# An attention and expert kernel: written order for its transfers, another opening, and another engine for the last sums

## The chip, the cores and the metric

The kernel runs on one core of a Trainium2 chip. The metric is the device time of one execution in microseconds (us). Three runs of the kernel before took 4551.12 to 4552.34 us, with a median of 4551.49 us.

A core has five engines, each with an instruction queue of its own: TensorE (PE in the profile, its weight loads PEld), VectorE (DVE), ScalarE (ACT), GpSimd (POOL) and SyncE (SP), which here only issues transfers. ScalarE and GpSimd issue transfers too.

## The reference, cut to what matters

```python
xn = layernorm(x)                          # x: (4, 2048, 512) float32
q, k, v = split(xn @ w_qkv, 3)             # 16 heads of 32
q, k = (irfft(rfft(t) * sigmoid(mask_logits)) for t in (q, k))
attn = softmax(einsum('bhqd,bhkd->bhqk', q, k) / sqrt(32))
attention = einsum('bhqk,bhkd->bhqd', attn, v).reshape(B, S, 512) @ w_out + b_out
best = argmax(softmax(xn @ w_gate))        # 8 experts, 100 tokens each
expert = gate * (xn @ w_expert + b_expert) # for the tokens that find a place
return x + attention + expert
```

The filter of q and k is linear, so the kernel multiplies the q and k weights by a filter matrix once, at the start.

## The kernel before, in words

**Units of work.** A stage k (0 to 15) is one batch and one group of four heads: b = k // 4, group c = k % 4. A stage has four blocks of 512 queries (n), a block has eight windows (w), and a window takes two tiles of 128 keys, an even and an odd one. So there are 512 windows of four passes (two tiles, two pairs of heads u). In each pass of the main loop (L844 to L892) TensorE does `shift` (L593: adds minus the row maxima, `negm`, into a PSUM bank by a bf16 matmul), the matmuls of one item of the maxima of a later block (`max_matmuls`, L446), and `scores` (L582). ScalarE takes the exponential into the tile `even` or `odd`, and VectorE reduces the maxima (`max_reduce`, L458, into `part`). `products` (L609) of the tile before multiplies by the values, and VectorE adds them into `num`.

**Maxima.** They run 40 items ahead (MAX_AHEAD), that is ten windows; a block has 32 items. The first 40 are worked off in a prelude before window 0 (L728 to L744). The last item of block B (numbered through, 0 to 63) falls in window 8B-3. `max_negate` (L470) then makes `neg` on VectorE, and in window 8B-2 `max_close` (L475) transposes it on TensorE, copies it to `rest` on ScalarE, splits it on GpSimd into three bf16 rows (`row`; a cast, then twice a subtraction and a cast) and has SP write these into `negm` by three DMAs. Block B begins in window 8B and can't before that. After window 501 there are no maxima left.

**Row sums.** For the denominators, the odd tile of a window is added onto the even one by an accumulating DMA from GpSimd's queue at the start of the next window (`pair`, L833), and the even tile of the window before onto that by GpSimd in the window after (`add_to`, L836, two instructions). After a block, `close_steps` (L628) makes the row sums on TensorE (`fold`), sends them through memory so that 128 partitions share the reciprocal (`sums`, `few`, `inverse`, `factor`: SP's DMAs, with the reciprocal of `few` on VectorE), multiplies on GpSimd (`ot`), projects, copies to `y` on ScalarE and adds `y` to the output by an accumulating DMA from GpSimd's queue (`add`, ten windows after the block). The very last block is closed by `close_last` (L673).

**Order.** Steps other than the passes stand in an agenda, a list for each window (`plan`, L782); half of them run after the even tile, half after the odd one. From L724 on, TensorE, VectorE, ScalarE and GpSimd are wrapped in `InOrder` (L71), which keeps their instructions in the written order. SP is not, nor is anything in the opening: there the framework's scheduler chooses the order of the queue. A DMA that waits in a queue holds up those behind it.

**Hand-over.** The tokens of the next batch are read twice, in chunks of 1 MB. In stage c = 2 they are loaded, measured, given the bias `b_out` and stored to the output as its first sum. From the end of that stage on they are loaded again, normalized and turned into `xnT`, in stage c = 3. Both passes use the two `xs` buffers of the pool `chunks`. The weights of a stage (`wg`, one buffer) are loaded from `wd` at the end of the stage two before it.

**Opening.** ScalarE's queue issues the constants, the raw weights and the V part of `wd` (L128 to L181), then comes the sigmoid (L182). SP loads x, and the filtering of group 0 (`filter_weights`, L192), which goes through `wd` in memory and back, stands behind the first chunk (L690 to L702). The other three groups are filtered in the prelude.

Of the kernel before, what the change touches and what calls it, by code (L numbers as in the profile page):

```python
# [25 lines left out]
P = 128  # L26
# [75 lines left out]
def attention_and_top1_experts(ctx: ExitStack, tc: tile.TileContext, a: dict, out: bass.AP):  # L102
# [24 lines left out]

    freq = const.tile([2 * NF, 2, P], F32, name="freq")  # L128
# [4 lines left out]
    falling = const.tile([P, E], F32, name="falling")  # L133
    nc.scalar.dma_start(out=falling, in_=a["c_falling"])
    token = const.tile([P, NT], F32, name="token")
    nc.scalar.dma_start(out=token, in_=a["c_token"])
    mask = const.tile([2 * NF, 1], F32, name="mask")
    logit_col = a["L0_attn_mask_logits"].rearrange("(f o) -> f o", o=1)
    nc.scalar.dma_start(out=mask[0:NF], in_=logit_col)
    nc.scalar.dma_start(out=mask[NF : 2 * NF], in_=logit_col)  # L140
# [30 lines left out]
    wd = [dram1.tile([P, NR, 3, P], F32, name=f"wd{c}") for c in range(NG)]  # L171
    raw = {}
    for s in range(2):
        for g in range(NR // 2):
            if g == 0:
                both = probs(s == 1)
            raw[s, g] = both[:, g]
            nc.scalar.dma_start(out=raw[s, g], in_=w_qkv[:, 2 * g : 2 * g + 2, s * DM : (s + 1) * DM])
    for c in range(NG):
        cols = slice(2 * DM + c * P, 2 * DM + (c + 1) * P)  # L180
        nc.scalar.dma_start(out=wd[c][:, :, 2, :], in_=w_qkv[:, :, cols])  # L181
# [9 lines left out]
    on = SimpleNamespace(tensor=nc.tensor, vector=nc.vector, scalar=nc.scalar, gpsimd=nc.gpsimd)  # L191
    def filter_weights(c):  # L192
        for s in range(2):
            pt, pw = bank(), bank()
            for r in range(NR):
                on.tensor.transpose(
                    pt[:, r * P : (r + 1) * P], raw[s, r // 2][:, r % 2, c * P : (c + 1) * P], ident
                )
            if s == 0:
                both = probs(c == 1)  # L200
            wt = both[:, s]
            on.scalar.copy(wt[:, 0, :], pt)
            for r in range(NR):
                at = slice(r * P, (r + 1) * P)
                on.tensor.matmul(pw[:, at], lhsT=wt[:, 0, at], rhs=filt, start=True, stop=True)
            on.scalar.copy(wt[:, 1, :], pw)
            nc.sync.dma_start(out=wd[c][:, :, s, :], in_=wt[:, 1, :].rearrange("p (r n) -> p r n", r=NR))
# [4 lines left out]
    def token_stage(b):  # L212
# [6 lines left out]
        def load(n, name="xs"):  # L219
            held[n] = chunk(name)  # L220
            nc.sync.dma_start(out=held[n], in_=x[b, n])
# [9 lines left out]
        def first_sums(n):  # L231

            nc.sync.dma_start(out=o[b, n], in_=held[n])

        def scale(first=0, last=NT):
            at = slice(first, last)
            on.scalar.activation(rstd[:, at], mv[:, at, 1], AF.Sqrt, bias=eps[:, 0:1])
            on.vector.reciprocal(rstd[:, at], rstd[:, at])
            on.gpsimd.tensor_tensor(shift[:, at], mv[:, at, 0], rstd[:, at], ALU.mult)
            on.gpsimd.tensor_scalar(shift[:, at], shift[:, at], -1.0, None, ALU.mult)  # L240
# [138 lines left out]
    wg, wo = {}, {}  # L379

    def load_qkv_weights(k):
        wg[k] = weights.tile([P, NR, 3, P], F32, name="wg", bufs=1)
        nc.sync.dma_start(out=wg[k], in_=wd[k % NG])

    def load_out_weights(k):
        c = k % NG
        wo[k] = weights.tile([P, DM], F32, name="wo")
        nc.sync.dma_start(out=wo[k], in_=a["L0_attn_w_out"][c * P : (c + 1) * P, :])
# [86 lines left out]
    def max_close(k, n):  # L475

        pn = bank()[0 : HG * TQ, 0:P]
        on.tensor.matmul(pn, lhsT=negs.pop((k, n)), rhs=ident, start=True, stop=True)
        rest = small.tile([HG * TQ, P], F32, name="rest")
        row = small.tile([HG * TQ, 3, P], BF16, name="row", bufs=2)  # L480
        on.scalar.copy(rest, pn)
        on.gpsimd.tensor_copy(row[:, 0, :], rest)
        for i in (1, 2):
            on.gpsimd.tensor_tensor(rest, rest, row[:, i - 1, :], ALU.subtract)
            on.gpsimd.tensor_copy(row[:, i, :], rest)
        negms[k, n] = qkv.tile([P, QB], BF16, tag="negm", name="negm", bufs=3)
        for i in range(3):
            nc.sync.dma_start(out=negms[k, n][i::DH, :], in_=row[:, i, :])
# [4 lines left out]
    def expert_steps():  # L493


        def begin():
            w_exp = chunk("w_exp")
            nc.sync.dma_start(out=w_exp, in_=a["L0_ffn_w_expert"].rearrange("(r p) n -> p r n", p=P))
            b_exp = work.tile([P, DM], F32, tag="b_exp", name="b_exp", bufs=1)
            nc.sync.dma_start(out=b_exp, in_=a["L0_ffn_b_expert"].partition_broadcast(P))  # L500
            entries = small.tile([P, NTAB, ST, 2], F32, name="entries")
            for i, table in enumerate(tables):
                nc.sync.dma_start(out=entries[:, i], in_=table.rearrange("(t p) c -> p t c", p=P))
# [124 lines left out]
    def close_steps(k, n, num, acc):  # L628
# [4 lines left out]
        def fold():  # L633
            den = work.tile([P, QB], F32, tag="den", name="den", bufs=1)
            on.scalar.copy(den, row_sums([acc]))
            held["sums"] = scratch.tile([HG, QB], F32, name="sums")
            nc.sync.dma_start(out=held["sums"], in_=den[0::DH, :])


        def fetch():  # L640
            held["few"] = small.tile([P, HG * QB // P], F32, name="few", bufs=2)
            nc.sync.dma_start(out=held["few"], in_=held["sums"].rearrange("h (c e) -> (h c) e", e=HG * QB // P))

        def invert():
            on.vector.reciprocal(held["few"], held["few"])
            held["inverse"] = scratch.tile([HG, QB], F32, name="inverse")
            nc.sync.dma_start(
# [3 lines left out]
        def spread():  # L651
            held["factor"] = work.tile([P, QB], F32, tag="factor", name="factor", bufs=1)
            for h in range(HG):
                nc.sync.dma_start(
                    out=held["factor"][DH * h : DH * (h + 1)], in_=held["inverse"][h].partition_broadcast(DH)
                )
# [12 lines left out]

        steps = [(2, fold), (3, fetch), (4, invert), (5, spread), (7, divide)]  # L670
        return steps + [(8, result, 0), (8, result, 1), (9, result, 2), (9, result, 3), (10, add)]

    def close_last(k, n, num, tiles, y):  # L673
# [9 lines left out]
        for t in range(TQ):  # L683
            on.vector.tensor_tensor(y[:, t, :], y[:, t, :], project(k, ot, t), ALU.add)
            if t % 2 == 1:
                nc.sync.dma_start(out=o[b, n, :, t - 1 : t + 1, :], in_=y[:, t - 1 : t + 1, :])
# [3 lines left out]
    for n in range(NQ):  # L690
        tiles = range(n * TQ, (n + 1) * TQ)
        load(n, "y" if n == 2 else "xs")
        for i in tiles:
            measure(i)
        scale(tiles[0], tiles[-1] + 1)
        for i in tiles:
            normalize(i)
            if i % 2 == 1:
                turn(i - 1)
        if n == 0:  # L700
            filter_weights(0)
            load_qkv_weights(0)  # L702
# [17 lines left out]
    first_projections = projections(0)  # L720
    for step in first_projections[:2]:
        step()
    ahead, first_projections = first_projections[2:7], first_projections[7:]
    on.tensor, on.vector, on.scalar, on.gpsimd = (  # L724
        InOrder(tc, engine) for engine in (nc.tensor, nc.vector, nc.scalar, nc.gpsimd)
    )
    closing = {}
    for i, item in enumerate(stream[:MAX_AHEAD]):  # L728
        if i % 4 == 0 and ahead:
            ahead.pop(0)()  # L730
        if i % 10 == 9 and i < 30:
            filter_weights(i // 10 + 1)
# [6 lines left out]
        max_reduce(item, half)  # L739
        while full_blocks:  # L740
            closing[i + 2] = full_blocks.pop(0)
            max_negate(*closing[i + 2])
        if i in closing:
            max_close(*closing[i])  # L744

# [36 lines left out]
    def plan(k):  # L782
# [18 lines left out]
        if k + 2 < B * NG:  # L801
            at(start + GW - 1, load_qkv_weights, k + 2)
# [3 lines left out]
        if c == NG - 2 and b + 1 < B:  # L806

            at(start + 10, begin_stage, b + 1)
            for n in range(NQ):
                at(start + 11 + 4 * n, in_stage, 0, n)  # L810
                at(start + 18 + 4 * n, in_stage, 7, n)
            for i in range(NT):
                at(start + 13 + i, in_stage, 1, i)
                at(start + 14 + i, in_stage, 6, i)
            at(start + GW - 2, in_stage, 2)
            at(start + GW - 2, in_stage, 0, 0)
            at(start + GW - 1, in_stage, 0, 1)
# [18 lines left out]
    def add_to(tile, sum_before):  # L836
        for u in range(2):
            on.gpsimd.tensor_tensor(tile[:, u], tile[:, u], sum_before[:, u], ALU.add)

    pairs, adds = {}, {}  # L840
# [3 lines left out]
    for k in range(B * NG):  # L844
        plan(k)
        for n in range(NQ):
            num = work.tile([P, QB], F32, tag="num", name="num")
            tiles = {}
            for w in range(NW):
                even, odd = w * WIN, w * WIN + 1  # L850
                if window in pairs:
                    pair(*pairs.pop(window))
                if window in adds:
# [3 lines left out]
                for j in (even, odd):  # L857
# [14 lines left out]
                    while full_blocks:  # L872
                        block = full_blocks.pop(0)
                        max_negate(*block)
                        at(window + 1, max_close, *block)
                    if left:
                        products(*left)
                    left = k, n, j, tiles[j], num
                    for step in here[:cut] if j == even else here[cut:]:
                        step()  # L880
                last = (k, n) == (B * NG - 1, NQ - 1)
                if not last or w < NW - 1:
                    pairs[window + 1] = tiles[even], tiles[odd]
                    if 0 < w and not (last and w == NW - 2):
                        adds[window + 2] = tiles[even], tiles[even - WIN]
                if last and w == NW - 2:
                    y = chunk("xs")
                    nc.sync.dma_start(out=y, in_=o[B - 1, n])
# [4 lines left out]
    products(*left)  # L893
    for step in agenda[window]:
        step()
    close_last(k, n, num, [tiles[j] for j in (NT - 6, NT - 4, NT - 2, NT - 1)], y)
# [36 lines left out]
```

## Time and profile before

| what | value |
|---|---|
| median of three runs | 4551.49 us |
| the profiled execution's own time | 4547.31 us |
| its span, first to last instruction | 4545.5 us |
| mean granted TensorE clock | 0.984 |
| DMA moved | 708.87 MB, mean 156 GB/s |
| first maxima matmul | 63.52 us |
| first matmul of window 0 | 123.84 us |
| last `products` matmul ends | 4512.2 us |
| `few` reciprocal, 128x16, VectorE | 247 ns |
| `row` cast, 16x128, GpSimd | 284 ns |
| `rest` subtraction, 16x128, GpSimd | 418 ns |
| `even` addition, 128x1024, GpSimd | 2549 ns |
| max reduction, 128x1024, VectorE | 1220 ns |

In the lines of the profile, a time line has start, duration, engine, source line, operation, out<-in, the shape and the count of merged instructions; in brackets stands the idle time before it and what ended it. L82 is the line of the `InOrder` helper and stands for every pinned instruction, so one goes by tile names there. SPq, ACTq and so on are the queues as they issue transfers. PEclk is the clock that TensorE was granted, as a share of full speed.

### The profile page before, as it was taken

To read this page: it belongs to the slowest core of one execution; us is meant where nothing else is said; L and a number is where in the kernel's file an instruction comes from. 1 tells how busy PE (TensorE), PEld (TensorE's weight loads), DVE (VectorE), ACT (ScalarE), POOL (GpSimd) and SP (SyncE) were. 2 spreads that over 40 slices of the span, in tenths; PEclk is the share of its full clock that TensorE was granted. 3 is DMA by queue.
4 is the path that set the end of the run, shared out by engine and by line. 5 is a ranking of instruction groups with operands and counts; after the bars stand their busy time and mean duration, and the time that the engine had idled before them with its cause. 6 is when DMAs were issued, how large, how long until landed. Compare 5 with 4: busy or idle time off the path is not lost.

```text
span 4545.5 us, 106083 instructions
## 1 busy us (share of the span) xinstructions
PE 4381.8 (96%) x44390; PEld 1877.2 (41%) x44390; DVE 3099.6 (68%) x3609; ACT 2590.4 (57%) x4933; POOL 3002.4 (66%) x2082
## 2 busy tenths in 40 slices
PE   6999999989999999998999999998999999999997
PEld 3444443434434344443444434343343444434332
DVE  4666777765767777775667767776667766777772
ACT  3455565565555655556555555555655565555654
POOL 0477676755766766775577666776567665777666
PEclk9999999999999999999999999999999999999998
DMA  5587787877777878797677777788768776788787
GB/s 119 132 176 154 148 161 151 193 174 145 151 149 144 163 154 160 154 211 171 125 150 149 160 152 146 163 175 181 162 127 159 155 148 128 152 171 163 153 166 146
DMA packets 193231, 708.87 MB, mean 156 GB/s; under 512 B 47778, under 2 KB 54084, under 8 KB 127344
## 3 DMA queue, kind: packets, MB, share of 16 engines
q0 software_dynamic: 110576, 606.88, 68.4%
q1 hardware_dynamic: 77800, 91.56, 6.6%
q8 instruction: 347, 5.69, 0.5%
q10 hardware_dynamic: 4376, 3.67, 0.4%
q14 instruction: 132, 1.08, 0.1%
HBM read 77.09 MB, written 89.99 MB: 37 GB/s over the span
## 4 chain that ended last, share of the span: by engine, by line
PE 85%; DMA 7%; POOL 3%; issue 2%; ACT 2%; DVE 1%; ACTq 0%; POOLq 0%; SPq 0%; DVEq 0%
PE array L82 85%; DMA even<-odd 3%; POOL even L82 2%; DMA few<-sums 1%; DMA negm<-row 1%; ACT odd L82 1%; DMA sums<-den 1%; DVE part L82 1%; DMA wg<-wd 0%; POOL ot L82 0%; DMA wd<-in_L_attn_w_qkv_dram 0%; ACT even L82 0%; PE array L394 0%; POOL table L82 0%; ACT xs L82 0%
## 5 line engine op out<-in xcount | busy, mean ns | idle before, releaser
L82 DVE TENSOR_REDUCE part<-array 128x2 f32<-128x1024 f32 (+1 forms) x2308 | 2432.7, 1099 | 1222.0 <-PE array L82 1210.0
L82 POOL TENSOR_TENSOR even<-even 128x1024 f32<-128x1024 f32 x892 | 2171.4, 2549 | 236.0 <-DMA even<-odd 234.1
L82 PE MATMUL array<-k,q 32*128 32x512 f32 x8192 | 2228.0, 623 | 1.9 <-DVE part L82 1.9
L82 PE MATMUL array<-q,k 32*128 32x512 f32 x8192 | 2057.8, 596 | 0.0
L82 ACT ACTIVATE even<-array 128x512 f32<-128x512 f32 x2048 | 1065.5, 601 | 501.6 <-PE array L82 484.5
L82 ACT ACTIVATE odd<-array 128x512 f32<-128x512 f32 x2048 | 1060.3, 601 | 442.1 <-issue 236.6
L82 POOL DMA_DIRECT2D even<-odd x511 | 464.0, 908 | 1059.9 <-ACT odd L82 865.4
L82 PEld LDWEIGHTS array<-k,q 32*128 32x128 f32 x8192 | 811.1, 184 | 175.1 <-DVE num L82 74.1
L82 PE MATMUL array<-negm,ones_b 3*128 3x512 bf16 x4096 | 799.4, 383 | 53.0 <-DMA negm<-row 35.5
L82 PEld LDWEIGHTS array<-q,k 32*128 32x128 f32 x8192 | 751.2, 186 | 11.4 <-issue 2.5
L82 DVE TENSOR_TENSOR num<-num,array 128x512 f32<-128x512 f32 x960 | 650.5, 678 | 60.8 <-PE array L82 39.8
L82 PEld LDWEIGHTS <-ones_b 3*128 3x128 bf16 x4096 | 203.5, 92 | 934.0 <-issue 775.3
L82 PE MATMUL array<-even,v 128*32 128x512 f32 x4096 | 547.2, 606 | 15.5 <-ACT odd L82 15.4
L82 PE MATMUL array<-odd,v 128*32 128x512 f32 x4096 | 549.4, 607 | 3.1 <-ACT even L82 3.1
L82 PE MATMUL array<-xnT,wg 128*32 128x512 f32 x4032 | 456.7, 592 | 1.6 <-DVE part L82 1.0
L82 PE MATMUL array<-wo,ot 128*32 128x512 f32 x2048 | 260.1, 599 | 17.8 <-POOL ot L82 17.8
L82 PEld LDWEIGHTS array<-xnT,wg 128*32 128x32 f32 x4032 | 130.4, 110 | 300.9 <-issue 265.1
L82 PEld LDWEIGHTS array<-even,v 128*32 128x32 f32 x4096 | 80.8, 108 | 406.4 <-ACT odd L82 396.6
L82 PEld LDWEIGHTS array<-odd,v 128*32 128x32 f32 x4096 | 81.3, 108 | 399.5 <-ACT even L82 389.2
L82 PEld LDWEIGHTS array<-wg,xnT 128*32 128x32 f32 x8192 | 226.4, 110 | 40.4 <-issue 23.4
L82 ACT COPY y<-array 128x512 f32<-128x512 f32 x252 | 147.8, 587 | 162.7 <-PE array L82 162.6
L82 PE MATMUL array<-wg,xnT 128*32 128x128 f32 x8192 | 236.6, 273 | 0.9 <-issue 0.9
(141 smaller groups left out, 1366.2 us busy)
## 6 DMA issues: line engine op xcount, KB each, us to landing
even<-odd POOLq DMA_DIRECT2D x511, 1024.0 KB, 8.1
out_dram<-y POOLq DMA_DIRECT2D x63, 1024.0 KB, 12.7
xs<-in_L_attn_x_dram SPq DMA_DIRECT2D x31, 1024.0 KB
out_dram<-xs SPq DMA_DIRECT2D x16, 1024.0 KB
factor<-inverse SPq DMA_DIRECT2D x252, 64.0 KB
wg<-wd SPq DMA_DIRECT2D x16, 768.0 KB
wo<-in_L_attn_w_out_dram SPq DMA_DIRECT2D x16, 256.0 KB
negm<-row SPq DMA_DIRECT2D x192, 4.0 KB
```

The source lines that it names most:

```text
L82: done = act(*args, **kwargs)
```

## The change

- SP is pinned too: all its transfers in the main loop go through `on.sync`, wrapped in `InOrder` after the opening, and so stand in the written order.
- The opening is written anew, with the four computing engines pinned in it. ScalarE's queue first issues the mask and two constants; the raw weights go to SP, ahead of all four chunks of x. All four groups are filtered at once beside the loading of x, group 0 straight into `wg`. The turning of chunks 1 to 3 into `xnT` (six of the eight `turn` steps), and the last four normalize steps, move into the prelude.
- `max_close` ends with ScalarE's two copies and runs after the even tile of window 8B-2. The rest is `max_split`, which runs at the start of window 8B-1, after `pair` and before `add_to`. ScalarE instead of GpSimd makes the first of the three rows.
- The loads and stores of the hand-over get other windows; the weights are loaded one window earlier, the second chunk of the second reading two windows later.
- When no maxima are left, VectorE and not GpSimd adds the even tiles, three windows after the tile's own and not two. The block before the last closes without memory (`fold_here`: a reciprocal of 128x512 on VectorE) and earlier. In the last block the last four tiles go into the row sums each by itself, with the running sum of the others.

```diff
+    mask = const.tile([2 * NF, 1], F32, name="mask")
...
-            nc.scalar.dma_start(out=raw[s, g], in_=w_qkv[:, 2 * g : 2 * g + 2, s * DM : (s + 1) * DM])
-    for c in range(NG):
-        cols = slice(2 * DM + c * P, 2 * DM + (c + 1) * P)
-        nc.scalar.dma_start(out=wd[c][:, :, 2, :], in_=w_qkv[:, :, cols])
+            nc.sync.dma_start(out=raw[s, g], in_=w_qkv[:, 2 * g : 2 * g + 2, s * DM : (s + 1) * DM])
...
+    def filter_steps(c):
+        held = {}
+        def turned(s):
+            if s == 0:
+                held["wt"] = probs(c % 2 == 1)
+            pt = bank()
             for r in range(NR):
                 on.tensor.transpose(
                     pt[:, r * P : (r + 1) * P], raw[s, r // 2][:, r % 2, c * P : (c + 1) * P], ident
                 )
+            on.vector.tensor_copy(held["wt"][:, s, 0, :], pt)
+        def filtered(s):
+            pw = bank()
+            wt = held["wt"][:, s]
             for r in range(NR):
                 at = slice(r * P, (r + 1) * P)
                 on.tensor.matmul(pw[:, at], lhsT=wt[:, 0, at], rhs=filt, start=True, stop=True)
+            done = pw.rearrange("p (r n) -> p r n", r=NR)
+            if c == 0:
+                on.scalar.copy(wg[0][:, :, s, :], done)
+            else:
+                on.scalar.copy(wt[:, 1, :], pw)
+                nc.sync.dma_start(out=wd[c][:, :, s, :], in_=wt[:, 1, :].rearrange("p (r n) -> p r n", r=NR))
+        return [lambda f=f, s=s: f(s) for s in range(2) for f in (turned, filtered)]
...
+        on.scalar.copy(row[:, 0, :], pn)
         on.scalar.copy(rest, pn)
-        on.gpsimd.tensor_copy(row[:, 0, :], rest)
+        closed[k, n] = rest, row
+
+    def max_split(k, n):
+        rest, row = closed.pop((k, n))
         for i in (1, 2):
             on.gpsimd.tensor_tensor(rest, rest, row[:, i - 1, :], ALU.subtract)
             on.gpsimd.tensor_copy(row[:, i, :], rest)
         negms[k, n] = qkv.tile([P, QB], BF16, tag="negm", name="negm", bufs=3)
         for i in range(3):
-            nc.sync.dma_start(out=negms[k, n][i::DH, :], in_=row[:, i, :])
+            on.sync.dma_start(out=negms[k, n][i::DH, :], in_=row[:, i, :])
...
+        def fold_here():
+            held["factor"] = work.tile([P, QB], F32, tag="factor", name="factor", bufs=1)
+            on.vector.reciprocal(held["factor"], row_sums([acc]))
...
+        if (k, n) == (B * NG - 1, NQ - 2):
+            return [(3, fold_here), (4, divide), (5, result, 0), (5, result, 1), (6, result, 2), (6, result, 3), (7, add)]
...
+    load(0)
+    load(1)
+    load(2, chunk("y"))
+    load(3, probs(False).rearrange("p u h q -> p (u h) q"))
+    wg[0] = weights.tile([P, NR, 3, P], F32, name="wg", bufs=1)
+    nc.sync.dma_start(out=wg[0][:, :, 2, :], in_=w_qkv[:, :, 2 * DM : 2 * DM + P])
+    for c in range(1, NG):
+        cols = slice(2 * DM + c * P, 2 * DM + (c + 1) * P)
+        nc.sync.dma_start(out=wd[c][:, :, 2, :], in_=w_qkv[:, :, cols])
...
+    for i in range(2 * NG + 1):
+        if i < 2 * NG:
+            turned[i]()
+        if i > 0:
+            filtered[i - 1]()
+        if 2 * NG - TQ <= i < 2 * NG:
+            measure(i - 2 * NG + TQ)
+    nc.sync.dma_start(out=wd[0], in_=wg[0])
+    first_projections = projections(0)
+    scale(0, TQ, on.vector)
+    for i in range(TQ):
+        normalize(i)
+        measure(TQ + i)
+        if i % 2 == 1:
+            turn(i - 1)
+    scale(TQ, 2 * TQ, on.vector)
+    for i in range(TQ, 2 * TQ):
+        normalize(i)
+        measure(TQ + i)
+    first_projections[0]()
+    scale(2 * TQ, 3 * TQ, on.vector)
+    for i in range(2 * TQ, 3 * TQ):
+        if i == 3 * TQ - 1:
+            first_projections[1]()
+        normalize(i)
+        measure(TQ + i)
+    scale(3 * TQ, NT, on.vector)
...
+    ahead = {1: lambda: turn(4), 3: lambda: turn(6), 6: first_projections[2]}
+    ahead.update({9: lambda: turn(8), 11: lambda: turn(10), 14: first_projections[3]})
+    ahead.update({17: lambda: turn(12), 19: lambda: turn(14), 22: first_projections[4]})
+    ahead.update({28: first_projections[5], 33: first_projections[6]})
...
+    on.sync = InOrder(tc, nc.sync)
...
-            at(start + GW - 1, load_qkv_weights, k + 2)
+            at(start + GW - 2, load_qkv_weights, k + 2)
...
-            for n in range(NQ):
-                at(start + 11 + 4 * n, in_stage, 0, n)
-                at(start + 18 + 4 * n, in_stage, 7, n)
+            for n, (come, go) in enumerate(((11, 19), (15, 23), (20, 28), (24, GW))):
+                at(start + come, in_stage, 0, n)
+                at(start + go, in_stage, 7, n)
             for i in range(NT):
-                at(start + 13 + i, in_stage, 1, i)
-                at(start + 14 + i, in_stage, 6, i)
-            at(start + GW - 2, in_stage, 2)
+                at(start + 13 + i + i // 8, in_stage, 1, i)
+                at(start + 14 + i + i // 8, in_stage, 6, i)
+            at(start + GW - 1, in_stage, 2)
             at(start + GW - 2, in_stage, 0, 0)
-            at(start + GW - 1, in_stage, 0, 1)
+            at(start + GW + 1, in_stage, 0, 1)
...
                 if window in pairs:
                     pair(*pairs.pop(window))
+                if window in splits:
+                    max_split(*splits.pop(window))
                 if window in adds:
                     add_to(*adds.pop(window))
...
+                    if j == even and window in full:
+                        splits[window + 1] = full.pop(window)
+                        max_close(*splits[window + 1])
...
+                        due, engine = (2, on.gpsimd) if maxima else (3, on.vector)
+                        adds[window + due] = tiles[even], tiles[even - WIN], engine
...
+    add_to(*adds.pop(window))
...
-    close_last(k, n, num, [tiles[j] for j in (NT - 6, NT - 4, NT - 2, NT - 1)], y)
+    close_last(k, n, num, [tiles[j] for j in (NT - 4, NT - 3, NT - 2, NT - 6, NT - 1)], y)
```

In the diff `in_stage` 0 is load, 1 measure, 2 scale, 6 the bias and 7 the store; GW is 32, the windows of a stage, and NW 8, those of a block.

## The prediction

> **What bounds the kernel now.** I read the page first, then the busy times of short stretches, then the timeline of each stretch in which TensorE idles. The page:
>
> ```profile
> span 4545.5 us, 106083 instructions
> PE 4381.8 (96%) x44390; PEld 1877.2 (41%) x44390; DVE 3099.6 (68%) x3609; ACT 2590.4 (57%) x4933; POOL 3002.4 (66%) x2082
> ...
> POOL 0477676755766766775577666776567665777666
> PEclk9999999999999999999999999999999999999998
> ```
>
> TensorE (PE) is busy 96% of the span, so only its idle time (163.7 us) and its halved clock are to be won; no matmul is saved by this change. The stretches show where:
>
> ```profile
> core 0: us, PE busy (x) PEld busy (x) DVE busy (x) ACT busy (x) POOL busy (x), PEclk, DMA share, GB/s
> 0.00:30.40 30.40, 8.44 (x33) 6.59 (x34) 9.21 (x27) 6.75 (x10) 1.35 (x13) 1.00 1.10 215
> 30.40:50.80 20.40, 12.49 (x49) 7.19 (x52) 3.35 (x11) 13.89 (x26) 1.23 (x6) 0.58 0.88 221
> 63.50:123.80 60.30, 52.77 (x461) 26.03 (x459) 43.03 (x42) 11.41 (x20) 1.68 (x5) 0.97 0.10 28
> ...
> 940.50:951.80 11.30, 0.00 (x0) 0.02 (x1) 0.92 (x2) 0.16 (x1) 7.01 (x5) 0.71 1.01 238
> 951.80:955.40 3.60, 3.59 (x20) 2.03 (x20) 1.29 (x2) 1.09 (x2) 3.60 (x2) 0.50 0.89 184
> ...
> 993.70:1000.60 6.90, 0.00 (x0) 0.00 (x0) 1.35 (x3) 0.59 (x1) 6.50 (x4) 0.69 0.71 146
> 1000.60:1006.60 6.00, 5.97 (x28) 2.91 (x32) 3.81 (x5) 2.35 (x5) 3.22 (x2) 0.50 0.68 140
> ```
>
> The columns after PEclk are DMA share and GB/s. Four places lose time: the opening; the hand-over between two batches, where PE does nothing for 11.3 and 6.9 us and then runs at clock 0.50 (the same near 2042 and 3140); one 8.5 us gap at 4369; and the end. The timelines name the causes of the hand-over and of the end:
>
> ```profile
> 930.68 0.50 SPq L383 DMA_DIRECT2D wg<-wd  x1
> 934.70 0.38 SPq L221 DMA_DIRECT2D xs<-in_L_attn_x_dram  x1
> 937.75 2.79 SPq L488 DMA_DIRECT2D negm<-row  x3
> ...
> 951.81 0.61 PE L82 MATMUL array<-negm,ones_b 3*128 3x512 bf16 x2 [11.35 <-DMA negm<-row]
> ...
> 4495.33 0.25 DVE L82 RECIPROCAL few<-few 128x16 f32<-128x16 f32 x1 [10.17 <-DMA few<-sums]
> 4496.18 0.61 PE L82 MATMUL array<-negm,ones_b 3*128 3x512 bf16 x2 [6.22 <-DVE num L82]
> 4532.71 1.32 POOL L82 DMA_DIRECT2D out_dram<-y  x1 [3.99 <-ACT y L82]
> ```
>
> negm (12 KB in three DMAs) is queued on SP behind 1.75 MB of weights and tokens, and a block can't begin without it. At 4490 VectorE (DVE) stands on the reciprocal's `few`, with the sums TensorE needs queued behind it. And the block before the last adds its 1 MB so late that the program ends on it.
>
> [...] of a pair sum even<-odd (128 packets of 8 KB, 8 per engine, about 0.64 us each), a `few` DMA issued 2 to 4 us after its first packet gets its own first packet 4.9 us after that first packet, that is when the eight are through. [...] Here every gap from 2.97 us on was followed by it, of five gaps of 2.1 to 2.2 us two. [...] the 512-wide `num` add (one input in PSUM) takes 0.678 us.
>
> **Part by part.** Against the profiled execution's own 4547.3 us (span 4545.5); the median, 4551.5, is 4.2 above it.
>
> *Opening, -24.* Now ScalarE's queue issues four weight copies before the sigmoid, which starts at 21.84, and the filter follows. After: 2 MB of raw weights first on SP; at the 249 GB/s of the first 25 us that is 8.4 us, and 2.2 for issue and latency (the first 1 MB of x landed 5.7 us after its issue, 4.2 of them transfer): 10.6. Eight filter steps of 4 transposes (0.66, at 54.35) and 4 matmuls (1.17, at 78.06): 14.6, [...] Then ScalarE in order up to the q copy: table and square root 1.6, VectorE's reciprocal and shift 0.4, 4 normalize at 0.75, 4 copies at 0.55, two more scales at 0.7, 7 more normalize, 2 more copies: 15, and 3 for half-clock projections: first maxima at 46 instead of 63.5. The 40 maxima cost VectorE 40 x 1.16 = 46.4; beside them PE has 40 x 0.5 + 5 projections x 3.64 + 6 turns x 1.3 = 46. Eight PSUM banks couple the two, so between 47 and the 60.3 of today; I take 53.5. First window at 99.5 instead of 123.84: -24 (-34 to -14). The transfers of V weights and of wd, and the table fills, that SP now carries as well, stand behind x; first needed in window 5, they cost nothing unless SP reaches that far late (then up to 5).
>
> *Hand-over, -51.5.* Lost now: 11.3 + 6.9 idle and half of 3.6 + 6.0 at half clock = 23.0; the other two, read the same way, 20.6 and 22.9: 66.5. In written order the weights (window GW-2) and the first reload leave right after the factor DMAs, about 1.5 windows earlier than negm; the fourth store and second reload come after negm. wg and x0, 1.75 MB, beside pair sums are some 3 MB, 12.6 us at the 238 GB/s of the gap above, done about when the pair of the last window starts. The reload at GW+1 then waits for the store on SP (queued behind it: sums, few, inverse), but has a window before sums is due, so `few` lands before VectorE asks for it and the second gap goes. What is late next: negm behind the last pair, and the scale step, now one window nearer to normalize. I leave 5 per hand-over: 66.5 - 15 = 51.5 (30 to 62).
>
> *4369, -10.8.* SP stood 32.5 us on the y load, hoisted out of order (it issued at 4362.54), with sums behind it; in order it leaves at the end. Gap 8.5 + 2.3 for 4.5 us at half clock.
>
> *End, -24.* From the last block's start (4455.0) to its last product is 57.2: 6.2 + 1.1 idle, 4.1 + 2.8 lost to half clock, so 43 of PE work. Moved in: the other block's four projections, 3.5. Half clock at the start stays: 50.6. Then five row sums instead of four, 4.9; from there to the last output DMA 6.6 (4524.7 to 4531.2) and an assumed 4.5 to land: 66.6 against 90.5. The 16 adds of 1.2 us that VectorE takes over and the 512-wide reciprocal (up to four of the 0.85 us ones, 3.4) lie under PE: between 4464 and 4490 VectorE is busy 4.81 of 25.7 us. Without that cover they would cost up to 23.
>
> *The split of the maxima, +34 and +8.* This is the price of the change. ScalarE's extra 0.25 us copy per block hides under PE. But max_split now stands after pair on POOL and before add. Now the casts precede the pair: row DMAs leave first and land 1.3 us after the last issue. After: pair issues 0.46 us after ScalarE's last exp of window 8B-2 (or when POOL is free), its packets run from 1.46 to 6.6 us later; four POOL operations (0.42, 0.28, twice, with spacing 1.7) end 2.6 us after the pair's start, so the last rows arrive inside the pair and land when it is through: exp end + 0.46 + 6.8 + 0.46 for the semaphore = 7.7. From exp end to the next block's first matmul today takes 6.1 to 6.3 us where that window has no projection (every fourth block: 4, 8, 16, 20, ...), 6.3 to 7.4 in the blocks about a hand-over, over 9 elsewhere. So ten blocks lose about 1.9, ten others (11, 13, 15, 27, 29, 31, 43, 45, 47, 52) about 1.4: 33, and 1 for the clock: +34. It could be 0 if rows overtook the pair, and about 70 if each gap also halved the clock. In the last stage POOL is 2.5 to 3 us behind at blocks 60, 61 and 63: about 3 each and 1.5 at 62, less what it saves of two waits on `ot`: +8. add is 1.7 later, with nothing waiting on it within the window.
>
> Sum: -24 - 51.5 - 10.8 - 24 + 34 + 8 = -68.3. Own time 4479, on the median's scale **4483 us**.
>
> **Rivals.** (1) *Nothing is held behind the pair*: rows slip between its packets, as sums did at 372.6 (it landed 1 us after a pair began). For it: row 0 comes from ScalarE early. Against: the `few` records. Then +42 falls away: 4441. (2) *The loads only change places*: the second gap of each hand-over stays in another guise (9.5 us each, 29) and the opening gives 14: 4522. For it: 1 MB pairs take 123 GB/s throughout. Against: nothing else crowds windows 95 to 98 as now. (3) *Slower*: the split's delay at all blocks. The pair took 8.3 us of packets when a load ran beside it (869.9 to 878.3). If that were the rule, negm would come 3.1 us later still: 20 blocks at 1.7 + 3.1 + 1.7 of half clock = 130, some 40 more at 1.2 = 48; 178 instead of 34: 4551.5 - 68.3 + 144 = 4627. It turns the sign from about 70 more than my 34, a pair of some 6.8 us. Against: most pairs before a block took 5.2 to 5.8. That a written order fails to be kept is no rival: each engine's instructions are pinned.
>
> **Chances.** Forecast 0.50 (4460 to 4510), (1) 0.21, (2) 0.21, (3) 0.08. About 0.2% is what a measurement can tell from no change. Of (3), 0.01 lies within that. So faster 0.92, same 0.01, slower 0.07. The range takes (1) and (2) and the ends of opening and hand-over: 4430 to 4525; outside lie (3) and some 0.1 at the edges.
>
> **What would show it.** Right: the first window near 100 us; no wait of PE on negm over 5 us near the three hand-overs, none on VectorE behind `few`; DVE adds even<-even in the last 50 us, PE above 90% there; the last transfer an SP store. For the split: negm packets ending with the pair's, waits of PE on negm of 1 to 3 us at every fourth block. Wrong: no such waits (then rival 1), gaps over 5 us still at 900 to 1010 (rival 2), or waits at most of the 64 blocks with PEclk down across the page (rival 3).

## The result, and the profile after

The changed kernel takes **4519.62 us**, the median of four runs (4517.56 to 4522.99), beside 4551.91 us for the kernel before in the same runs. The ratio is 0.9928, with a 95% interval of 0.9914 to 0.9941: some 32 us faster, where 68 were forecast. The profiled execution took 4519.14 us, with a span of 4517.2.

The head of the page after:

```profile
span 4517.2 us, 106256 instructions
...
PE 4390.0 (97%) x44398; PEld 1883.0 (42%) x44398; DVE 3134.8 (69%) x3642; ACT 2596.8 (57%) x4988; POOL 2919.2 (65%) x1993
...
PEclk9999999999999999999999999999999999999999
```

POOL has lost 83 us of work and DVE taken on 35. TensorE's busy time has not fallen, though the page counts the same matmuls but for eight: some of them still run at half clock (110.1 us of it after the first 100), and the forty slices are too coarse to show where. The busy times of short stretches, in the opening and about the first hand-over, show it better (the columns are those of the prediction's table):

```profile
core 0: us, PE busy (x) PEld busy (x) DVE busy (x) ACT busy (x) POOL busy (x), PEclk, DMA share, GB/s
0.00:27.60 27.60, 15.54 (x106) 13.95 (x106) 11.77 (x27) 9.86 (x15) 0.90 (x11) 0.98 0.93 315
27.60:46.00 18.40, 15.61 (x100) 5.97 (x100) 10.40 (x28) 11.84 (x20) 0.00 (x0) 0.75 0.96 98
46.00:96.70 50.70, 49.72 (x441) 21.08 (x440) 40.58 (x44) 12.91 (x23) 1.39 (x4) 1.00 0.02 3
...
924.00:934.00 10.00, 4.82 (x38) 2.41 (x35) 3.59 (x6) 4.38 (x8) 7.66 (x7) 0.86 0.88 238
989.00:1005.00 16.00, 13.65 (x112) 6.07 (x108) 10.53 (x11) 10.38 (x19) 13.55 (x12) 0.89 0.84 172
```

TensorE works for 15.5 us of the first 27.6, where it had 8.4 us in the first 30.4. At the hand-over 10 us hold 4.8 of work and 16 hold 13.7, in place of two stretches with none. The new loss is in the waits for `negm`. Each line gives the microseconds in total, the number of waits and the longest; first those of the kernel before, then those of the changed one:

```profile
DVE few L82 <- DMA few<-sums: 63.6, 13, 10.2
PE array L82 <- DMA negm<-row: 35.5, 5, 11.4
```

```profile
DVE few L82 <- DMA few<-sums: 4.1, 3, 1.9
PE array L82 <- DMA negm<-row: 70.5, 22, 7.0
PEld L82 <- DMA negm<-row: 45.2, 11, 7.9
```

VectorE's waits on `few` are nearly gone. TensorE's waits on `negm` were 35.5 us in 5 places before, three hand-overs and little else. Now they are twice as long and in 22 places. I call the start of a block's first `negm` matmul its *start*. Comparing starts in the two traces splits the 28.3 us by which the spans differ. Each row is the change over a stretch:

| stretch | forecast | measured |
|---|---|---|
| opening, to block 0's start | -24 | -27.1 |
| three hand-overs, block 11 to 13, 27 to 29, 43 to 45 | -51.5 | -13.2 - 15.6 - 15.9 = -44.7 |
| blocks 61 to 62 (the gap at 4369) | -10.8 | -5.1 |
| block 63 to the end | -24 | -24.8 |
| all other stretches | +42 | +14.2 + 15.3 + 23.1 + 15.8 + 5.0 = +73.4 |
| sum | -68.3 | -28.3 |

The +42 holds some 6 us for blocks 13, 29, 45 and 62, which the table counts in other rows. So most of the gains came nearly as forecast, and the split of the maxima cost far more. The experiments ask why.

### The profile page after: what moved, and what is told of

Its sections match the earlier page's. It is cut to its first block, busy times and chain, and to the rows that moved or that the text cites. A ratio compares the mean times of both kernels' runs of the same rounds, so it can differ in the third digit from the quotient of the medians.

```text
span 4517.2 us, 106256 instructions
## 1 busy us (share of the span) xinstructions
PE 4390.0 (97%) x44398; PEld 1883.0 (42%) x44398; DVE 3134.8 (69%) x3642; ACT 2596.8 (57%) x4988; POOL 2919.2 (65%) x1993
## 5 line engine op out<-in xcount | busy, mean ns | idle before, releaser
L82 POOL TENSOR_TENSOR even<-even 128x1024 f32<-128x1024 f32 x876 | 2118.2, 2517 | 183.0 <-DMA even<-odd 181.8
L82 POOL DMA_DIRECT2D even<-odd x510 | 442.0, 867 | 1227.6 <-ACT odd L82 1032.7
L82 PE MATMUL array<-negm,ones_b 3*128 3x512 bf16 x4096 | 799.1, 384 | 78.7 <-DMA negm<-row 70.5
L82 DVE TENSOR_TENSOR num<-num,array 128x512 f32<-128x512 f32 x960 | 651.2, 678 | 50.5 <-PE array L82 31.2
L82 PEld LDWEIGHTS array<-even,v 128*32 128x32 f32 x4096 | 81.1, 108 | 406.4 <-ACT odd L82 393.5
```

Source lines behind the costliest of these rows:

```text
L82: done = act(*args, **kwargs)
```

## The experiments

The theory: `negm`'s rows, issued after the pair sum, land when its packets are through; the weights `wg`, which the written order of SP puts just ahead, delay them more; and behind gaps so lengthened TensorE runs at half clock (0.50 behind the 4.64 us ahead of block 36). Rival A: what delays the rows is the place on GpSimd, not the packets. Rival B: the written order of SP isn't what cures the hand-over, the new windows are. Every kernel was timed four or five times beside the kernel before, whose median was 4549.79 to 4552.7 us.

**e1: the split ahead of the pair sum.**

```diff
-                if window in pairs:
-                    pair(*pairs.pop(window))
                 if window in splits:
                     max_split(*splits.pop(window))
+                if window in pairs:
+                    pair(*pairs.pop(window))
```

> The changed kernel with max_split ahead of pair on GpSimd at the start of a window; nothing else differs. Theory (the rows of negm land only when the pair's packets are through, since the pair is queued first): the first matmul of most blocks no longer waits on negm, the waits at blocks 1, 16, 32, 60, 61, 63 go, and the time falls by 40 to 60 us against the changed kernel, to about 4460 to 4480. Where the weights are issued just ahead of negm (blocks 8, 20, 24, 36, 40, 52, 56) waits of 1 to 3 us stay. Rival (it is the written order of the SP queue, that is the weights and factor DMAs ahead of negm, and not the pair): within 10 us of 4519.6.

Measured: **4443.09 us** (4437.3 to 4448.16), ratio 0.9768 (0.9754 to 0.9781), 76 us less than the change as it stands (73 by the ratios). That is more than the 40 to 60 expected, and the waits of 1 to 3 us expected where the weights stand just ahead are not there. First the timeline of the changed kernel ahead of block 36, then that of e1 at the same place:

```profile
2580.71 0.75 SPq L82 DMA_DIRECT2D wg<-wd  x1
2581.50 2.49 SPq L82 DMA_DIRECT2D negm<-row  x3
...
2581.26 0.84 POOL L82 DMA_DIRECT2D even<-odd  x1
...
2583.16 0.28 POOL L82 CAST row<-rest 16x128 bf16<-16x128 f32 x1
...
2591.47 0.61 PE L82 MATMUL array<-negm,ones_b 3*128 3x512 bf16 x2 [4.64 <-DMA negm<-row]
```

```profile
2541.55 0.37 SPq L82 DMA_DIRECT2D wg<-wd  x1
2541.97 2.33 SPq L82 DMA_DIRECT2D negm<-row  x3
...
2543.47 0.28 POOL L82 CAST row<-rest 16x128 bf16<-16x128 f32 x1
2543.97 0.88 POOL L82 DMA_DIRECT2D even<-odd  x1 [0.22 <-issue]
...
2547.95 0.39 PE L82 MATMUL array<-negm,ones_b 3*128 3x512 bf16 x2
```

In the first, the last row is made at 2583.44 and TensorE has it at 2591.47, 8 us later. The packet records give the reason: the pair's packets ran from 2585.47 to 2591.20, and the last 28 of the rows' 48 only from 2590.52 to 2590.77. In e1 the weights still leave 0.42 us ahead of `negm`, but the pair leaves after it, and the block begins with no wait. What is left of the waits in e1:

```profile
PE array L82 <- DMA negm<-row: 0.8, 1, 0.8
```

The page of e1 has:

```profile
span 4441.3 us, 106256 instructions
PE 4360.2 (98%) x44398; PEld 1867.7 (42%) x44398; DVE 3130.3 (70%) x3642; ACT 2596.1 (58%) x4988; POOL 2941.8 (66%) x1993
```

So two sums make up the 75.9 us between the spans. TensorE's idle time (span less busy time) falls from 127.2 to 81.1 us, by 46. Its busy time falls from 4390.0 to 4360.2 us, by 30, with as many matmuls: that is the clock, for the time at half clock after the first 100 us goes from 110.1 to 38.5 us. So the clock had two fifths of the gain.

**e2: the weights one window earlier, the split left where the change has it.**

```diff
-            at(start + GW - 2, load_qkv_weights, k + 2)
+            at(start + GW - (3 if k and c < NG - 2 else 2), load_qkv_weights, k + 2)
```

> The changed kernel with the weights of stages that follow c = 0 and c = 1 issued one window earlier (GW-3), which puts them ahead of the factor DMAs; the pair stays ahead of the split. Theory: 768 KB of weights no longer stand between the last factor DMA and negm, the pair's packets start 1.5 us after its issue as at other blocks and not 2.5 to 4.2 us after; waits at blocks 8, 20, 24, 36, 40, 52, 56 shrink from 2.5 to 4.6 us to about 1.8 and stop halving the clock: 20 to 30 us less than 4519.6. Rival (the pair alone delays negm, the weights are noise): less than 8 us of change.

Measured: 4503.38 us, ratio 0.9897 (0.9882 to 0.9912), some 14 us less than the change by the ratios. That is less than the 20 to 30 expected and more than the rival's 8; the trace is of the slowest of the four runs (4511.69 us). The gaps ahead of blocks 8, 20, 24, 36, 40 and 52 go from 3.38, 3.43, 3.82, 4.64, 3.67 and 2.52 to 1.88, 2.00, 2.50, 2.00, 1.85 and 0.99 us. That ahead of 56 grew from 3.53 to 7.47: there an add on GpSimd stood 5.67 us on an earlier pair sum, and the last row was made late, at 3983.93. What I had wrong is the clock: five of the six shortened gaps, all but the 0.99, were still followed by 3.4 us at half clock, and the time at half clock after the first 100 us only fell from 110.1 to 103.9 us. The weights' place is part of the cost, and what remains is the pair.

**e3: both edits.**

> Both edits together: split ahead of pair, and the weights one window earlier. Theory: nearly all of the 73 us that the blocks outside the hand-overs lost against the kernel before come back: 60 to 75 us less than 4519.6, about 4445 to 4460, with PE waits on negm left only at the three hand-overs. Rival (part of the 73 us has another cause, such as the order of SP's reloads or the clock): it stays above 4475.

Measured: 4452.99 us, ratio 0.9791 (0.9778 to 0.9805), 10 us more than e1. With the rows ahead of the pair sum, moving the weights has nothing left to win. More than half of the excess lies at the first hand-over, behind a wait of 3.94 us on `negm` ahead of block 12 that e1 does not have. e9 below has the same wait (4.00 us) without this edit, so the edit need not be its cause.

**e4: the kernel before with the late split alone**, SP left to the scheduler, the opening, hand-over and end as before. The edit is the split of `max_close` into `max_close` and `max_split`, with the second after `pair`.

> The kernel before with one part of the change alone: max_close after the even tile of window 8B-2 with two ScalarE copies, and max_split at the start of window 8B-1 between pair and add_to. SP stays unpinned. Theory: 30 to 50 us slower than before (4551.9), by waits on negm of 1 to 2.5 us at the blocks whose last window is short (4, 8, 13, 15, 16, 20 and so on), and not by as much as the changed kernel lost, since the weights leave earlier here. Rival (the late split costs nothing by itself; pinning SP is what costs): within 8 us of 4551.9.

Measured: **4606.11 us**, ratio 1.0119 (1.0103 to 1.0134): 55 us slower than the kernel before, where 30 to 50 were expected. TensorE waits 84.5 us on `negm` in 26 places, against 35.5 in 5. This is the cost without the written order. Here the scheduler keeps the weights away from `negm`, and the seven blocks 8, 20, 24, 36, 40, 52 and 56 show 1.4 to 2.2 us each, 13.4 together, where the change has 25.0. So 1.9 us is the pair's own delay, as forecast, and the other half at these blocks comes from the two edits together. But even without the weights the split costs more than my 42: the gaps at the last four blocks grow by 15.5 us, and the half clock after the first 100 us from 127.7 to 166.5 us.

**e5: a small pair sum.** The order of the change, but in the windows with a split the pair sum moves only 64 of 2048 columns and so leaves most of the odd tile out of the row sums.

```diff
+        if part:
+            first, second = first[:, 0, 0, 0:64], second[:, 0, 0, 0:64]
...
-                    pair(*pairs.pop(window))
+                    pair(*pairs.pop(window), part=window in splits)
```

> The changed kernel with its order kept (pair sum first, split after it), but in the windows that have a split the pair sum's DMA moves only 64 of the 2048 columns of the tile (so at 64 of 512 pair sums most of the odd tile is left out). The instruction still takes GpSimd its 0.84 us. Theory, that the rows of negm are held by the packets of the pair sum: the 32.5 us of gaps ahead of negm at blocks 4, 8, 16, 20, 24, 32, 36, 40, 48, 52 and 56 fall below 8 and the time comes to 4440 to 4460. Rival one, that what counts is the place on GpSimd (0.84 us of issue ahead of four operations): the gaps stay above 15 and the time above 4490. Rival two, that the 768 KB weight load just ahead on SP is enough by itself: the gaps at 8, 20, 24, 36, 40, 52 and 56 (25.0 us) stay, those at 4, 16, 32 and 48 (7.5 us) go, and the time is about 4490.

Measured: 4431.94 us, ratio 0.9743 (0.973 to 0.9757). The pair sum still takes its 0.83 us of GpSimd ahead of the four operations, and the weights still stand just ahead on SP; only bytes are gone. The waits of PE on `negm` fall from 70.5 us in 22 places to 6.1 in 2, at blocks 61 and 63:

```profile
PE array L82 <- DMA negm<-row: 6.1, 2, 4.6
```

Over the stretches in which the change lost 73.4 us against the kernel before, this kernel loses 3.4. Rival A falls, and so does the idea that the weights hold the rows by themselves: without the bytes of the pair sum they cost no wait at these blocks. This kernel also moves fewer bytes, at 64 of 512 pair sums, so e1, not this run, gives the size.

**e6: e1 with SP's order left to the scheduler.**

```diff
-    on.sync = InOrder(tc, nc.sync)
```

> e1 (split ahead of the pair sum) with SP's order left to the scheduler instead of written. Theory, that the written order of SP is what cures the hand-over: the gaps of some 10 us in front of blocks 12, 28 and 44 come back and each hand-over costs 15 to 25 us more, 4490 to 4515 in all. Rival, that the new windows of weights, stores and reloads do it alone: within 10 us of e1's 4443.

Measured: 4501.62 us, ratio 0.9894 (0.9879 to 0.991), 58 us more than e1. The first hand-over, in its timeline and its stretches:

```profile
908.32 0.33 SPq L668 DMA_DIRECT2D few<-sums  x1
...
914.29 0.25 DVE L82 RECIPROCAL few<-few 128x16 f32<-128x16 f32 x1 [11.46 <-DMA few<-sums]
...
915.68 0.58 PE L82 MATMUL array<-negm,ones_b 3*128 3x512 bf16 x1 [7.32 <-DVE part L82]
```

```profile
908.40:915.80 7.40, 0.12 (x4) 0.12 (x4) 1.50 (x3) 0.00 (x0) 5.47 (x3) 0.72 0.73 145
915.80:922.60 6.80, 6.80 (x37) 2.87 (x39) 5.24 (x8) 2.17 (x4) 0.26 (x1) 0.55 0.49 157
```

VectorE stands 11.46 us on `few` with the maxima queued behind it; TensorE idles 7.3 us, then runs at clock 0.55. From block 11's start to 13's e6 takes 2.7 us more than the kernel before; e1 takes 21.3 less. At the other two hand-overs e6 takes 8.0 and 4.4 us less, e1 19.2 and 21.4. So without the written order the new windows earn some 10 of e1's 62 us. The gaps of some 10 us ahead of blocks 12, 28 and 44 that I expected did not come back (3.2, 4.5 and 3.4 us); the larger losses stand behind `few`, in gaps of TensorE of 7.3, 4.1, 3.2 and 7.2 us. The `y` load is hoisted again too (it left at 4341.31), VectorE then stands 9.67 us on a `few`, and TensorE has a gap of 8.55 us at 4348.

**e7: e1 with the old windows of the hand-over**, SP in written order: weights at GW-1, `scale` at GW-2, reloads at GW-2 and GW-1, stores seven windows after their loads.

```diff
-            at(start + GW - 2, load_qkv_weights, k + 2)
+            at(start + GW - 1, load_qkv_weights, k + 2)
...
-            for n, (come, go) in enumerate(((11, 19), (15, 23), (20, 28), (24, GW))):
-                at(start + come, in_stage, 0, n)
-                at(start + go, in_stage, 7, n)
+            for n in range(NQ):
+                at(start + 11 + 4 * n, in_stage, 0, n)
+                at(start + 18 + 4 * n, in_stage, 7, n)
```

> e1 with the hand-over's old windows (weights at GW-1, scale at GW-2, reloads at GW-2 and GW-1, stores seven windows after their loads) under the written order of SP. Theory, that the written order is what counts: some 5 to 15 us more than e1, 4448 to 4458. Rival, that the windows count: the two gaps of each hand-over come back in part, 4480 to 4510.

Measured: **4435.79 us** (4432.87 to 4438.8), ratio 0.975 (0.9737 to 0.9763). The three hand-overs earn 22.9, 19.3 and 23.5 us over the kernel before, e1's 21.3, 19.2 and 21.4. So the written order does it, and under it the new windows earn nothing: rival B falls. Whether they are a small loss is open: e7 is 7 us faster than e1, but e9 below shows differences of that size where an edit doesn't reach.

**e8: e1 with the adds left on GpSimd to the end.**

```diff
-                        due, engine = (2, on.gpsimd) if maxima else (3, on.vector)
+                        due, engine = 2, on.gpsimd
```

> e1 with the adds of the running sums kept on GpSimd to the end, one window earlier (due 2 instead of 3); four tiles are still folded at the end. Theory, that GpSimd is what is late in the last 60 us: the end is 6 to 15 us longer, 4449 to 4458. Rival, that VectorE's adds only change places, since GpSimd has 35 of 46 us of work there anyway and the fold of four tiles brings the gain: within 4 us of e1.

Measured: 4457.25 us (4449.0 to 4461.1), ratio 0.9793 (0.978 to 0.9807), 11 to 14 us more than e1. From block 63's start to the end it takes 77.7 us, e1 67.9; the change and e2, e3, e5, e6 and e7, with the same end as e1, take 64.6 to 66.3. In the main stretch of that block in e8, below, GpSimd is busy 40 of 57 us and TensorE idles 7. That is one gap, at 4415: TensorE waits for `ot`, which stands on GpSimd behind an add that waited 5.66 us for its pair sum.

```profile
4383.00:4440.00 57.00, 49.71 (x377) 13.28 (x378) 12.85 (x15) 35.60 (x69) 40.24 (x24) 0.89 0.81 164
```

Another 6 us lie at the second hand-over, with a gap of 4.1 us in a stretch that the edit doesn't reach: the kernels differ by some microseconds there, whatever the edit at the end.

**e9 and e11: block 61 also folded in place**, in e1 and in e7.

```diff
-        if (k, n) == (B * NG - 1, NQ - 2):
+        if k == B * NG - 1 and n in (NQ - 3, NQ - 2):
```

> e1, and the denominators of block 61 are inverted in place by VectorE as those of block 62 are, instead of going through memory. In e1 VectorE stands 6.1 us on the few of block 61 and TensorE 5.0 us behind it (at 4350.7), then at half clock. Theory: a reciprocal of 3.36 us in its place takes that gap away, 4 to 7 us less than e1. Rival: the reciprocal, 3.1 us longer than the small one, delays the last maxima just as much, within 2 us of e1.

> e7 (split first, written order of SP, old windows at the hand-over) with block 61 folded in place as in e9. If e7's 5.0 us gap at 4285.5 goes with it, some 5 us less than e7, 4428 to 4433; if not, within 2 us of e7.

Measured: e9 4451.24 us, ratio 0.9782 (0.9768 to 0.9795), against e1's 0.9768; e11 4438.85, ratio 0.9756 (0.9742 to 0.9769), against e7's 0.975. No gain. In e9 the 5.0 us gap at 4350 is gone, but one of 7.05 us has come inside block 63, at 4401.9. There one of VectorE's adds waits 8.89 us for the pair sum's DMA, with `num` behind it. From block 61's start to the end e1 and e9 both take 189.2 us: the wait only moved. All of e9's excess over e1, 8 us by the medians, lies ahead of that, where the edit doesn't reach. So a difference of some microseconds between two of these kernels counts here only where it lies in the stretch that the edit changes.

**e10: e1 with block 62's denominators through memory**, and so with its closing steps as late as before.

```diff
-        if (k, n) == (B * NG - 1, NQ - 2):
+        if k < 0:
```

> e1 with block 62's denominators through memory as in the kernel before; the adds on VectorE and the fold of four tiles stay. Theory, that this block's late 1 MB add is what the program before ended on: the end is 8 to 20 us longer, 4451 to 4463, and the last instruction is GpSimd's add to memory. Rival, that VectorE's adds earn the end: within 4 us of e1.

Measured: 4459.69 us, ratio 0.9802 (0.9789 to 0.9815), some 15 us more than e1, 11.4 of them after block 63's start (79.3 us against 67.9). Its last DMA is again the add to memory:

```profile
4441.55 1.85 SPq L82 DMA_DIRECT2D out_dram<-xs  x2
...
4444.90 1.31 POOL L82 DMA_DIRECT2D out_dram<-y  x1 [3.98 <-ACT y L82]
```

## Why the prediction was wrong, step by step

**Opening, right.** Forecast -24, measured -27.1. The first maxima began at 42.0 us, not 46, and the prelude took 54.7, not 53.5. Some 3 us of the 46 were an allowance of mine for a slower clock in the filter, which no trace shows: the changed kernel filters from 9.18 to 22.31 us, and the clock, on record from 12.9 us on, was 1.00 there. Its projections did begin at half clock (0.50 from 31.71 to 36.83 us).

**Hand-over, right in size, wrong in one reason.** Forecast -51.5, measured -44.7, in which the split's waits at blocks 13, 29 and 45 (5.9 us) are contained; without them -50.5. The signs named for it came: no wait on `negm` there over 3.6 us, and hardly one on `few`. I credited the new windows along with the written order. e6 and e7 show the written order alone.

**The gap at 4369, right in its cause, half in size.** In order, the `y` load left at 4448.26 and no longer held `sums`; before, SP had stood 32.5 us on it. Measured were -5.1, with 3.1 us of `negm` gap inside; in e1, which has no such gap there, -7.4.

**End, right.** From block 63's start to the end I had 66.6 us; it took 65.6. The end of the changed kernel:

```profile
4474.11 3.36 DVE L82 RECIPROCAL factor<-array 128x512 f32<-128x512 f32 x1 [0.18 <-PE array L82]
...
4502.73 2.35 DVE L82 TENSOR_TENSOR even<-even 128x1024 f32<-128x1024 f32 x2
...
4511.71 1.93 SPq L82 DMA_DIRECT2D out_dram<-xs  x2
```

Two adds take 2.35 us, 1.2 each, as in the prediction; the trace of before has no such add on VectorE, only its max reduction of that width, at 1.22. The reciprocal takes 3.36, where four 128-wide ones took 3.39 before (at 4524.79). The program ends on a store from SP, 3.6 us after the last issue, where I had assumed 4.5. e8 and e10 divide it: about 10 us for VectorE's adds and 11 for the fold in place with its earlier steps; the fold of the last four tiles wasn't tried by itself.

**The split of the maxima, wrong.** This is the step that failed: "+34 and +8", of which some 36 us belong to the ordinary stretches, became +73 over them. Its mechanism, rows that land with the pair's last packet, is what e1 and e5 show; what failed is the size. Here are these stretches together, first before, then after:

```profile
sum 3813.72, PE 3783.60 PEld 1629.20 DVE 2686.95 ACT 2199.76 POOL 2613.50; mean PE 756.72 PEld 325.84 DVE 537.39 ACT 439.95 POOL 522.70
sum 3887.17, PE 3810.51 PEld 1643.77 DVE 2689.31 ACT 2205.36 POOL 2577.88; mean PE 762.10 PEld 328.75 DVE 537.86 ACT 441.07 POOL 515.58
```

TensorE's idle time grew from 30.1 to 76.7 us, by 46.5. Its busy time, for the same work, grew by 26.9. Against these stand 35 us of gaps and 1 us of clock in my sum. So the clock is the larger miss. Three terms were too small, and part of one too large:

- *The pair's start.* I let its packets begin 1.46 us after its issue, as in the kernel before. That held where the weights weren't near: blocks 4, 16, 32 and 48 lost 1.77, 2.27, 1.85 and 1.65 us, against my 1.9. That the 1.9 fits is partly luck, for my own figures give less: 7.7 less 6.1 to 6.3 is 1.5. The blocks began 7.3 to 8.0 us after the pair's issue, where the sum has 7.2. At blocks 8, 20, 24, 36, 40, 52 and 56 the 768 KB of weights had just left, and their packets ran ahead of the pair's or among them: at block 36 those of the weights ran from 2582.09 to 2586.12, and those of the pair began 4.2 us after its issue. At these seven blocks the gaps were 3.6 us on average. The prediction put the weights "about 1.5 windows earlier than negm"; at block 36 they left 0.8 us before it. In written order they stand behind the four factor DMAs, and left right behind them (2576.84 to 2580.61 at block 36). I costed the move of the weights and the delay of the split apart, each against the kernel before, and not against each other. At the blocks about a hand-over it was the other way. I gave them 1.4 us each, but six blocks (11, 15, 27, 31, 43 and 47) did not wait for `negm` at all, and my 6.3 to 7.4 us would have given 1.4 at most.
- *The clock.* I gave it 1 us. Here is the stretch of block 4's gap and what follows, then that of block 36:

```profile
387.17:388.94 1.77, 0.00 (x1) 0.03 (x1) 0.94 (x2) 0.18 (x1) 1.60 (x2) 1.00 0.44 88
388.94:396.00 7.06, 7.06 (x68) 3.10 (x72) 4.87 (x6) 4.38 (x9) 7.05 (x5) 1.00 0.56 113
2586.83:2591.47 4.64, 0.01 (x1) 0.03 (x1) 0.94 (x2) 0.18 (x1) 3.07 (x3) 0.84 1.03 212
2591.47:2596.80 5.33, 5.33 (x28) 2.41 (x32) 2.45 (x2) 2.17 (x4) 4.33 (x2) 0.50 0.75 154
```

  The gap of 1.77 us left the clock at 1.00; after the 4.64 us the next 5.3 us ran at 0.50 and did 28 matmuls, about half as many a microsecond. Over the ordinary stretches the time at half clock grew from 11 to 80 us. TensorE worked in 10 and 71 us of it, and half of the difference, 30, is enough for the 26.9. In the traces of before, after and e1 every gap from 3.07 us on was followed by half clock, as far back as the clock is on record (from 30.4 us in before, 12.9 in the changed kernel); so were about 19 of the 49 gaps between 1.6 and 3.03 us. (The gap of 2.97 us, from which on the prediction has half clock follow, lay within a stretch at half clock already.) So some gaps of 1.8 to 3 us cost clock too, and e2 shows it: taking the weights away made the gaps shorter, but most of them still brought half clock, 3.4 us of it where it had been 3.4 to 6.8. e1, with hardly a wait on `negm`, still has +15.7 us over these stretches, 5.0 of them a gap behind `few` at 4350.
- *The last stage.* I gave blocks 60 to 63 about 8 us. Their gaps were 4.13, 4.97, 3.07 and 7.04, against 0.37, 0, 0 and 3.31 before: 15.5 us more.

**The rivals.** (1) is refuted by the 22 waits, (2) by the hand-over, though its number, 4522, comes nearest to the time measured, (3) since some 40 blocks have no gap ahead of them. What came was between the forecast and (3): few blocks, but each of them dear.

## What to carry to other kernels

A small transfer that an engine's next block waits for belongs ahead of a large one, even when the two are in different queues: here three rows of 4 KB issued after a 1 MB accumulating DMA, and not ahead of it, cost 76 us. Two moves that are each costed against the old schedule have to be costed against each other, for a load that the one brings forward can meet the transfer that the other puts back. And a stall of TensorE cost more than its own length here: price it with the half clock, which in these traces followed every gap on record from 3.07 us on and many from about 1.8.

The version to take is e7: written order for SP, the new opening and end, the split ahead of the pair sum, and the old windows of the hand-over. At 4435.79 us it takes 2.5% less than the kernel before.

## What the runs showed of the hardware that I had not expected

- At the same place, 0.84 us of a DMA's issue on GpSimd cost no wait and its 1 MB, behind the weights, a wait of 4.6 us (the change at block 36, and e5).
- A gap of 3.03 us (at 175.1 in the changed kernel) wasn't followed by half clock, one of 1.94 us (at 3024.3) was: between 1.6 and 3.03 us the length alone doesn't decide. But for the last piece of a run, half clock comes in pieces of 3.4 us and their multiples in all three traces; at the gap of 4.64 us it lasted 6.8 (2590.00 to 2596.83).
- VectorE's 1024-wide add took 1.2 us; at 4477.93, where GpSimd multiplies `ot`, two took 4.09 us. Whether that is the other engine's doing wasn't tried.
